# A hybrid block: spare banks for the last scores, one visit for the output projection, and block transposes moved from TensorE to VectorE and DRAM

## The chip, the cores and the metric

The kernel runs on one core of a Trainium2 chip. The metric is device microseconds of that core, from one launch; a time is the median of several runs. Five engines work beside each other, each with its own instruction queue: TensorE (PE in the profile; its weight loads are listed as PEld), VectorE (DVE), ScalarE (ACT), GpSimd (POOL) and SyncE (SP), which here only issues DMAs.

## The reference, cut to what matters

Input x has 2 sequences of 2048 tokens of 256 features, all float32. Four layers follow each other, each on the normalized x and added to it:

```python
x = x + attention_a(layernorm(x))   # 16 heads of 16 features, 4 for keys and values, softmax
x = x + ffn(layernorm(x))           # "rotations"
x = x + attention_b(layernorm(x))   # linear and causal, 16 heads, rotary, gate, norm, projection
x = x + ffn(layernorm(x))           # "rotations", the second time, the same weights
```

The core of attention_a is `softmax(q k / 4) v` and a projection `out @ Wo + bo`. The core of ffn is

```python
gf = global_net(x.mean(over tokens))          # one number a sequence
out = x
for _ in range(3):
    tf = coupling_net(out)                     # one number a token
    coupling = 0.1 + range * (0.7 * gf + 0.3 * tf - 0.5) * 2
    out = out + coupling * twist(out)
return out
```

So ffn needs its input feature by feature for the matmuls, and, before anything else can be scaled, the sum of its input over a sequence.

## The kernel before, in words

The tokens stay in SBUF as `xs`: 32 tiles of 128 tokens by 256 features. A second buffer, `zq` (128 partitions, 2 halves of the features, 4096 tokens), holds the transposed input of whatever layer needs it by features. The tokens are cut into 8 blocks of 512 (`NB`, `BLK`), four to a sequence.

**Attention a** (`attention_a`, from line 153) works in 32 units: block j and one of four groups of heads g. For a unit, `largest` (line 361) first computes all scores with queries on the partitions, 64 banks of 128x512 (`s`, line 376), and VectorE takes the maximum of each bank (line 380). Later the unit's scores are computed again with keys on the partitions (`p`, `score`, line 643), a second matmul subtracts the maxima (`shift`, line 649), ScalarE takes the exponential (line 655), and `weigh` (line 630) multiplies by the values. The generator `largest` runs 80 banks (`LEAD`) ahead of this second pass. The main loop (line 637) goes over 32 units x 16 steps kb; each step draws four banks of maxima from `largest` and handles four scores r = 0 to 3. PSUM has 8 banks: 3 for the maxima's `s` (pool `pss`), 4 for `p` (`psp`), 1 for the weighted sum (`pav`). As the maxima run ahead, they end before the second pass does, in unit 30 at kb = 12.

`finish(u, av)` (line 459) is a generator too: the loop calls it once a step (lines 667 and 684), and it handles the unit just ended, in small portions. For the last group of a block (g = 3) it ends with the output projection: two banks `po` of eight matmul records each (line 499), and VectorE's add to `xs` (line 504), with a `yield` after each bank, so that the two lie in two neighbouring steps.

**Behind it** (`behind`, line 721): first rotations, attention b, second rotations. All instructions of PE, VectorE, ScalarE and GpSimd keep the order of the program here (`in_order(begin)`, line 1419); the DMAs on SP are not bound by that. All PSUM tiles but one come from one pool of 7 banks (`bank`, line 740).

Attention b goes block by block (the loop from line 1329), software-pipelined by hand: x is the current block, y the next, `before` the previous. Each block has four quarters of 128 tokens: `energies(t)` multiplies keys and queries into four banks `pe` (line 1114) and VectorE masks them into `en` (line 1120); `output(t)` multiplies the state (line 1131) and then `en` by the values (line 1140). `project_out(h)` projects half a block, transposes it for statistics (`pog`, line 993) and lets VectorE compute them (lines 106 to 110); `add_out(h)` adds the result to `xs` (line 1180).

The inputs of the second rotations are made here too, one block late: `next_look` computes the normalization's statistics, `next_norm` (line 1188) writes the normalized tokens into `fzt`, and `next_turn` (line 1192) transposes them. `turn` (line 126) does this with eight PE transposes of 128x128 into two banks (line 131), and ScalarE copies each bank into `zq` while it adds the sum over the tokens into `sums1` (`accum_out`, line 1196; an activation and a read of the accumulator). `next_turn` of the previous block is the last thing in an iteration; the next thing on all engines is `x.energies(0)` of the next block. The last block's own `next_turn` comes after the loop.

`context(b)` (line 774), drawn by `next(front)` in iteration NB - 2 for the first sequence and by `next(front1)` behind the loop for the second, adds up `sums1` and computes the global network. The second rotations then read `zq`.

Of the kernel before, what the change touches and what calls it, by code (L numbers as in the profile page):

```python
# [9 lines left out]
F32 = mybir.dt.float32  # L10
F32R = mybir.dt.float32r
AF = mybir.ActivationFunctionType
# [4 lines left out]
P = 128  # L17
B, N, D = 2, 2048, 256
T = B * N
BLK = 512  # L20
NB = T // BLK
BPB = N // BLK
KB = N // P
# [44 lines left out]
def tile_hybrid(ctx: ExitStack, tc: tile.TileContext, x: bass.AP, consts: bass.AP, wa_d: bass.AP, wf_d: bass.AP, wb_d: bass.AP, out: bass.AP):  # L68
    nc = tc.nc
# [8 lines left out]
    zq = keep.tile([P, 2, T], F32, name="zq")  # L78

    own = ctx.enter_context(tc.tile_pool(name="own", bufs=1))  # L80
    dram = ctx.enter_context(tc.tile_pool(name="a_dram", bufs=2, space=bass.MemoryType.DRAM))
# [15 lines left out]
    def tokens(j):  # L97
        return xs[:, 4 * j : 4 * j + 4, :]
# [54 lines left out]
    def attention_a():  # L153
        with ExitStack() as st:
# [20 lines left out]
            pss = st.enter_context(tc.tile_pool(name="a_s", bufs=3, space=PSUM))  # L175
            psp = st.enter_context(tc.tile_pool(name="a_p", bufs=4, space=PSUM))
# [168 lines left out]
            units = [(j, g) for j in range(NB) for g in range(G)]  # L345
# [113 lines left out]
            def finish(u, av):  # L459

                j, g = units[u]
                m, e = g // 2, 64 * (g % 2)
                avs = own.tile([P, BLK], F32, tag="swap", name=f"avs{u}", bufs=2)
                nc.scalar.copy(avs, av)
                if g == 0:
                    tc.keep_in_program_order(
                        nc.gpsimd.tensor_tensor(
                            tokens(j), tokens(j), bo_row.unsqueeze(1).to_broadcast([P, 4, D]), ALU.add
                        )
                    )  # L470
                    outs[j] = [own.tile([P, 2, BLK], F32, tag=t, name=f"{n}{j}") for t, n in (("og", "oc"), ("kt", "sums"))]
                oc, sums = outs[j]

                ds, dr = (dram.tile([KV, BLK], F32, tag=t, name=f"{t}{u}") for t in ("ds", "dr"))
                nc.sync.dma_start(ds, avs[16:P:32, :])
                rs = own.tile([P, 16], F32, tag="rs", name=f"rs{u}", bufs=2)
                nc.sync.dma_start(rs, ds.rearrange("r (p x) -> (r p) x", x=16))
                for r in range(KV):
                    nc.sync.dma_start(oc[e + 16 * r : e + 16 * r + 16, m, :], avs[32 * r : 32 * r + 16, :])
                for _ in range(5):  # L480
                    yield
                tc.keep_in_program_order(nc.vector.reciprocal(rs, rs))
                nc.sync.dma_start(dr.rearrange("r (p x) -> (r p) x", x=16), rs)
                for r in range(KV):
                    nc.sync.dma_start(
                        sums[e + 16 * r : e + 16 * r + 16, m, :], dr[r : r + 1, :].to_broadcast([16, BLK])
                    )
                for _ in range(3):
                    yield
                if g % 2 == 1:  # L490
                    nc.gpsimd.tensor_tensor(oc[:, m, :], oc[:, m, :], sums[:, m, :], ALU.mult)  # L491
                yield
                if g == G - 1:
                    for i in range(2):
                        po = bank(f"po{j}_{i}")
                        for t in range(2):
                            tok = slice((2 * i + t) * P, (2 * i + t + 1) * P)
                            for h in range(2):
                                mm(  # L499
                                    po[:, t * D : (t + 1) * D], oc[:, h, tok], wo[:, h, :],  # L500
                                    start=(h == 0), stop=(h == 1),
                                )
                        pair = tokens(j)[:, 2 * i : 2 * i + 2, :]
                        nc.vector.tensor_tensor(pair, pair, po.rearrange("p (t d) -> p t d", t=2), ALU.add)
                        yield

            LEAD, WARM = 64 + 16, 6
            ahead = largest()
# [3 lines left out]
            at = {n: tuple(a - _WA["wk"][0] for a in _WA[n]) for n in ("wk", "bk", "wv", "bv")}  # L512
# [124 lines left out]
            for u, kb in ((u, kb) for u in range(len(units)) for kb in range(KB)):  # L637
                if (u, kb) == (0, 4):
                    in_order(begin, (engines.PE,))
                qP, mrow = queries[u], mrows[u % 2]  # L640
                k0 = units[u][0] // BPB * N + kb * P
                t, es = [], []

                def score(r):
                    row = slice(64 * (r % 2), 64 * (r % 2) + 64)
                    t.append(psp.tile([P, BLK], F32, tag="p", name=f"p{u}_{kb}_{r}"))
                    mm(t[r], kP[r // 2][row, k0 : k0 + P], qP[r // 2][row, :], start=True, stop=False)  # L647

                def shift(r):
                    row = slice(64 * (r % 2), 64 * (r % 2) + 64)  # L650
                    mm(t[r], pick[row, :], mrow[r // 2][row, :], start=False, stop=True)  # L651

                def exp(r):
                    es.append(sb.tile([P, BLK], F32, tag="e", name=f"e{u}_{kb}_{r}", bufs=8))
                    nc.scalar.activation(es[r], t[r], AF.Exp, scale=1.0 / HD**0.5)  # L655


                next(ahead, None)
                next(ahead, None)
                score(0)  # L660
                score(1)
                shift(0)
                shift(1)
                exp(0)
                exp(1)
                if kb == 1:
                    next(done, None)
                score(2)
                next(ahead, None)
                score(3)  # L670
                shift(2)
                next(ahead, None)
                shift(3)
                exp(2)
                exp(3)
                if last is not None:
                    if last[1] == 0:
                        av = pav.tile([P, BLK], F32, tag="av", name=f"av{last[0]}")
                    weigh(*last)
                    if last[1] == KB - 1:  # L680
                        done = finish(last[0], av)
                last = u, kb, es
                if kb > 1:
                    next(done, None)
                    next(norms, None)
                if u % G == 1 and kb == 1 and G < u < 4 * G:
                    norms = norm(u // G - 1)
                if kb == 4 and u + 2 < len(units):
                    project(u + 2)()
                if rest is not None and next(rest, "end") == "end":  # L690
                    rest = None
                    loads.close()
                    late = later_pools["late"] = ctx.enter_context(tc.tile_pool(name="late", bufs=1, side="right"))
                    for n, (name, of) in enumerate((("wf", wf_d), ("wb", wb_d))):
                        weights[name] = late.tile([P, of.shape[1]], F32, name=name)
                        nc.sync.dma_start(weights[name], of)
                    for name in ("w4", "b3"):
                        at = slice(*_WF[name])
                        nc.sync.dma_start(weights["wf"][64:P, at], wf_d[0:64, at])
# [21 lines left out]
    def behind(tail):  # L721
        wf, wb = weights["wf"], weights["wb"]
        late = later_pools["late"]
# [199 lines left out]
        sums1 = hold.tile([P, 2, NB], F32, name="sums1")  # L923
# [72 lines left out]
        class Block:  # L996
# [19 lines left out]
            def turn(self):  # L1016
                j = self.j
                self.z = take("z", [P, 2, BLK], f"bz{j}")
                turn(self.zt, lambda c: bank(f"bztr{j}_{c}"), lambda c, tr: nc.scalar.copy(self.z[:, c, :], tr))
# [170 lines left out]
                scale(self.fzt, self.tile_of, *self.scales)  # L1190

            def next_turn(self):
                j = self.j
                turn(
                    self.fzt, lambda c: bank(f"ztr1_{j}_{c}"),
                    lambda c, tr: nc.scalar.activation(
                        zq[:, c, j * BLK : (j + 1) * BLK], tr, AF.Copy, accum_out=sums1[:, c, j : j + 1]
                    ),
                )


        blocks = [Block(j) for j in range(NB)]
# [21 lines left out]
        f = rotations(0, sums0, False)  # L1224
        context, first, second, third, fourth, _ = f
# [100 lines left out]
        f = rotations(1, sums1, True)  # L1326
        context, first, second, third, fourth, turn_ahead = f
        front, front1 = context(0), context(1)
        for j, x in enumerate(blocks):
# [28 lines left out]
            x.energies(2)  # L1358
            if before:
                before.next_norm()  # L1360
            if j == NB - 2:
                next(front)
            if y:
# [35 lines left out]
        fourth(0)  # L1399
        first(2, 1)  # L1400
        third(1)
        x.next_turn()
        next(front1)
        second(2)
# [134 lines left out]
```

## Time and profile before

| what | us |
|---|---|
| median of 3 runs (2105.64 to 2108.85) | 2107.24 |
| the profiled execution | 2107.98 |
| its span, first to last instruction | 2106.2 |
| PE busy | 2085.9 |
| DVE busy | 1697.6 |
| ACT busy | 1427.5 |
| POOL busy | 355.2 |

The profile comes from one execution. Its busy times overlap, as the engines work beside each other; matmuls are pipelined, so that PE counts as busy in small waits too. The granted TensorE clock was 0.997 over the span. In time, attention a takes the span up to about 1510 us, the first rotations up to about 1695 (the first projection for attention b is at 1682), attention b from there to about 1955, and the second rotations the rest. Lines of a timeline give start, duration, engine, line, operation, tiles (out<-in), shapes and how many were merged; in brackets, how long the engine had been idle and who ended that. A group's duration in such a line is from its first start to its last end.

### The profile page before, as it was taken

Reading aid. Unit: us, or ns where it says so; the run is one execution under the profiler, and the core shown is the slowest. Engines: PE = TensorE matmul, PEld = TensorE weight load, DVE = VectorE, ACT = ScalarE, POOL = GpSimd, SP = SyncE. Lnnn points to the kernel's source line nnn. Section 1 sums busy time; section 2 is a strip of 40 time slices with the busy share of each in tenths; the row PEclk is TensorE's granted clock in tenths of the full one; section 3 lists DMA queues with packets and bytes.
Section 4 is the critical chain, followed back from the end, with each engine's and each line's share of the span. In section 5 each row is a group of like instructions: output and inputs, shape, how many; then the busy total and the mean of one; then the engine's idle time right before and its main releaser. Section 6 shows DMA issues by size and latency. Waiting matters only on the chain.

```text
span 2106.2 us, 38754 instructions
## 1 busy us (share of the span) xinstructions
PE 2085.9 (99%) x14158; PEld 1011.4 (48%) x14158; DVE 1697.6 (81%) x3241; ACT 1427.5 (68%) x2787; POOL 355.2 (17%) x352
## 2 busy tenths in 40 slices
PE   9999999999999999999999999999999999999998
PEld 4444444444444444444444444444444567776434
DVE  7999988998998998999899899987134678886336
ACT  4477777777777777787777777778864445554443
POOL 3100010000001000000000000000135355542451
PEclk9999999999999999999999999999999999999999
DMA  6511010110101011010110101100100000000002
GB/s 199 149 44 40 18 37 19 48 38 19 38 18 48 10 50 37 18 48 10 47 40 18 43 15 47 40 17 8 53 1 1 0 2 1 1 1 2 1 0 80
DMA packets 59696, 68.72 MB, mean 33 GB/s; under 512 B 24944, under 2 KB 34032, under 8 KB 59248
## 3 DMA queue, kind: packets, MB, share of 16 engines
q1 hardware_dynamic: 58592, 64.79, 11.2%
q8 instruction: 111, 1.82, 0.4%
q10 hardware_dynamic: 720, 0.92, 0.1%
q14 instruction: 81, 0.66, 0.1%
q0 software_dynamic: 192, 0.52, 0.1%
HBM read 35.78 MB, written 26.21 MB: 29 GB/s over the span
## 4 chain that ended last, share of the span: by engine, by line
PE 95%; DVE 2%; DMA 1%; ACT 1%; issue 0%; POOL 0%; SPq 0%; DVEq 0%; ACTq 0%; POOLq 0%
PE av L632 24%; PE s L376 23%; PE p L647 12%; PE q1f L814 8%; PE p L651 7%; PE q2f L824 4%; PE pe L1114 2%; PE bpo L1140 2%; PE po L499 1%; PE pq L972 1%; PE pw L981 1%; PE pv L981 1%; PE pk L972 1%; PE q3f L836 1%; PE pq L336 1%; DVE mx L380 1%
## 5 line engine op out<-in xcount | busy, mean ns | idle before, releaser
L380 DVE TENSOR_REDUCE mx<-s 128x1 f32<-128x512 f32 x2048 | 1273.7, 682 | 104.5 <-PE s L376 97.7
L655 ACT ACTIVATE e<-p 128x512 f32<-128x512 f32 x2048 | 1057.5, 603 | 314.1 <-PE p L651 307.4
L376 PE MATMUL s<-a_kP,qP 64*128 64x512 f32 x2048 | 706.5, 470 | 3.9 <-DVE mx L380 2.0
L651 PE MATMUL p<-a_m,a_pick 64*128 64x512 f32 x2048 | 585.3, 415 | 0.0
L376 PEld LDWEIGHTS s<-a_kP,qP 64*128 64x128 f32 x2048 | 283.6, 184 | 566.1 <-DVE mx L380 528.2
L632 PE MATMUL av<-e,a_v 128*32 128x512 f32 x4096 | 545.9, 605 | 0.0
L647 PE MATMUL p<-qP,a_kP 64*128 64x512 f32 x2048 | 525.7, 394 | 2.5 <-ACT e L655 2.5
L647 PEld LDWEIGHTS p<-qP,a_kP 64*128 64x128 f32 x2048 | 286.7, 185 | 65.2 <-ACT e L655 25.4
L651 PEld LDWEIGHTS p<-a_m,a_pick 64*128 64x128 f32 x2048 | 283.7, 184 | 25.8
L814 PE MATMUL q1f<-zq,wf 128*128 128x512 f32 x384 | 176.1, 601 | 0.0
L632 PEld LDWEIGHTS av<-e,a_v 128*32 128x32 f32 x4096 | 81.0, 108 | 128.6 <-issue 120.5
L398 POOL TENSOR_TENSOR mt<-nm,mt 128x16 f32<-128x16 f32 x31 | 6.9, 221 | 733.7 <-ACT mt L397 733.7
L815 ACT ACTIVATE a1f<-q1f,wf 128x512 f32<-128x512 f32 x96 | 65.8, 686 | 94.6 <-PE q1f L814 91.4
L814 PEld LDWEIGHTS q1f<-zq,wf 128*128 128x128 f32 x384 | 70.2, 190 | 96.9 <-issue 85.3
L1120 DVE TENSOR_TENSOR en<-pe,small 128x512 f32<-128x512 f32 x128 | 79.4, 681 | 15.0 <-PE pe L1114 15.0
L855 DVE TENSOR_SCALAR cf<-cf,f_beta,alphaf 128x512 f32<-128x512 f32 x32 | 32.7, 1023 | 67.6 <-ACT cf L854 67.6
L824 PE MATMUL q2f<-a1f,wf 128*128 128x512 f32 x192 | 87.0, 595 | 0.0
L237 POOL TENSOR_TENSOR ql<-zq,qh 128x512 f32<-128x512 f32 x15 | 19.3, 1284 | 364.6 <-ACT qh L234 364.6
L859 POOL TENSOR_TENSOR tf<-cf,zq 128x512 f32<-128x512 f32 x32 | 56.6, 1768 | 102.4 <-DVE cf L855 101.9
L826 ACT ACTIVATE a2f<-q2f,wf 128x512 f32<-128x512 f32 x48 | 32.6, 685 | 56.2 <-PE q2f L824 56.2
L861 POOL TENSOR_TENSOR zq<-zq,tf 128x512 f32<-128x512 f32 x32 | 56.8, 1776 | 2.5
L491 POOL TENSOR_TENSOR oc<-oc,sums 128x512 f32<-128x512 f32 x16 | 20.6, 1288 | 209.6 <-DMA sums<-dr 138.2
(209 smaller groups left out, 1634.3 us busy)
## 6 DMA issues: line engine op xcount, KB each, us to landing
qP<-dq SPq DMA_DIRECT2D x64, 256.0 KB
dq<-qh SPq DMA_DIRECT2D x62, 128.0 KB
dq<-ql SPq DMA_DIRECT2D x62, 128.0 KB
a_kP<-dk SPq DMA_DIRECT2D x16, 256.0 KB
oc<-avs SPq DMA_DIRECT2D x128, 32.0 KB
sums<-dr SPq DMA_DIRECT2D x128, 32.0 KB
out<-xs SPq DMA_DIRECT2D x16, 256.0 KB
xs<-in_x SPq DMA_DIRECT2D x7, 512.0 KB
```

What stands on the lines that cost most here:

```text
L376: mm(s, qP[r // 2][row, qi * P : (qi + 1) * P], kP[r // 2][row, k0 + kb * BLK : k0 + (kb + 1) * BLK], start=True, stop=True,)
L380: nc.vector.tensor_reduce(mx[:, r, qi : qi + 1, kb], s, AX.X, ALU.max)
L632: mm(av[32 * r : 32 * r + 32, :], vA[:, units[u][0] // BPB * KB + kb, 32 * r : 32 * r + 32], es[r], start=(kb == 0), stop=(kb == KB - 1),)
L647: mm(t[r], kP[r // 2][row, k0 : k0 + P], qP[r // 2][row, :], start=True, stop=False)
L651: mm(t[r], pick[row, :], mrow[r // 2][row, :], start=False, stop=True)
L655: nc.scalar.activation(es[r], t[r], AF.Exp, scale=1.0 / HD**0.5)
L814: mm(q1, w1[:, c, m * P : (m + 1) * P], z[:, c, :], start=(c == 0), stop=(c == 1))
L815: nc.scalar.activation(a1[:, m, :], q1, AF.Gelu, bias=b1[:, m : m + 1])
L824: mm(q2, w2[:, c, :], a1[:, c, :], start=(c == 0), stop=(c == 1))
L859: nc.gpsimd.tensor_tensor(t1, cs, z[:, 0, :], ALU.mult)
L861: nc.gpsimd.tensor_tensor(z[:, 1, :], z[:, 1, :], t1, ALU.subtract)
L1120: nc.vector.tensor_tensor(self.ens[t][w], pes[w].rearrange("p (h n) -> p h n", h=4), const("triu").unsqueeze(1).to_broadcast([P, 4, P]), A ...
```

## The change

Three edits. First, the `yield` after each bank `po` of the output projection moves out of the loop, so that both banks are done in one step. Second, once the maxima are done, the scores with odd r take their bank from the maxima's pool. Third, for the blocks 0 to 6, `next_turn` no longer uses PE: VectorE transposes 128 tokens by 256 features in squares of 32x32 within one instruction; 16 DMAs (one per 128 tokens and 32 partitions) write the squares to a DRAM tile in the right places, in runs of 32 elements; two DMAs bring it back into `zq`. The squares lie in a ring of three buffers. The sums over the tokens, which came with ScalarE's copy out of the banks, are now made by a ScalarE copy of `zq` onto itself, `next_sum`, one iteration later (for block 6 behind the loop). Block 7 is transposed as before.

```diff
@@ finish @@
                         nc.vector.tensor_tensor(pair, pair, po.rearrange("p (t d) -> p t d", t=2), ALU.add)
-                        yield
+                    yield
@@ score @@
-                    t.append(psp.tile([P, BLK], F32, tag="p", name=f"p{u}_{kb}_{r}"))
+                    spare = r % 2 == 1 and LEAD + 4 * (u * KB + kb) >= 64 * len(units)
+                    pool, tag = (pss, "s") if spare else (psp, "p")
+                    t.append(pool.tile([P, BLK], F32, tag=tag, name=f"p{u}_{kb}_{r}"))
@@ Block @@
             def next_turn(self):
                 j = self.j
+                if j + 1 < NB:
+                    to = dram.tile([D, BLK], F32, tag="dz", name=f"dz{j}")
+                    at = to.rearrange("(b f) (t a i) -> t a f b i", f=32, a=4, i=32)
+                    for t in range(4):
+                        square = late.tile([P, D], F32, tag="square", name=f"square{j}_{t}", bufs=3)
+                        nc.vector.transpose(square, self.fzt[:, t, :])
+                        for a in range(4):
+                            nc.sync.dma_start(
+                                at[t, a], square[32 * a : 32 * a + 32, :].rearrange("f (b i) -> f b i", i=32)
+                            )
+                    for c in range(2):
+                        nc.sync.dma_start(
+                            zq[:, c, j * BLK : (j + 1) * BLK], to[c * P : (c + 1) * P, :]
+                        )
+                    return
                 turn(
...
+            def next_sum(self):
+                for c in range(2):
+                    z = zq[:, c, self.j * BLK : (self.j + 1) * BLK]
+                    nc.scalar.activation(z, z, AF.Copy, accum_out=sums1[:, c, self.j : self.j + 1])
@@ the loop over the blocks of attention b @@
             if before:
                 before.next_norm()
+            if j > 1:
+                blocks[j - 2].next_sum()
@@ behind that loop @@
         third(1)
+        blocks[NB - 2].next_sum()
         x.next_turn()
```

## The prediction

> **What bounds the kernel now.** I read the page first: the busy rows, then the chain that ended last.
>
> ```profile
> PE   9999999999999999999999999999999999999998
> DVE  7999988998998998999899899987134678886336
> PE 95%; DVE 2%; DMA 1%; ACT 1%; issue 0%; POOL 0%; SPq 0%; DVEq 0%; ACTq 0%; POOLq 0%
> ```
>
> The chain is TensorE (PE) almost throughout, so work taken from PE pays, but a wait added to VectorE (DVE) costs only where PE then waits for it. A busy PE in these rows can hide waits, so I read the three stages in the timeline.
>
> Behind the last maxima (1464 to 1510 us), an inner step alternates:
>
> ```profile
> 1464.76 4.18 ACT L655 ACTIVATE e<-p 128x512 f32<-128x512 f32 x8
> 1466.06 0.50 PE L647 MATMUL p<-qP,a_kP 64*128 64x512 f32 x2
> 1466.87 0.18 PEld L647 LDWEIGHTS p<-qP,a_kP 64*128 64x128 f32 x1 [0.29 <-ACT e L655]
> 1468.52 0.50 PE L647 MATMUL p<-qP,a_kP 64*128 64x512 f32 x2
> 1469.35 4.18 ACT L655 ACTIVATE e<-p 128x512 f32<-128x512 f32 x8 [0.41 <-PE p L651]
> 1470.64 0.50 PE L647 MATMUL p<-qP,a_kP 64*128 64x512 f32 x2
> ```
>
> Steps start 2.46 and 2.12 us apart (the step before these starts at 1463.94, 2.12 earlier). In the long one the third score waits for a bank that the exponentials still hold; then ScalarE (ACT) idles 0.41.
>
> The output projection, here for one batch of tokens:
>
> ```profile
> 1370.43 2.00 PE L499 MATMUL po<-a_wo,oc 128*128 128x256 f32 x8
> 1372.36 0.51 PE L376 MATMUL s<-a_kP,qP 64*128 64x512 f32 x2
> 1372.47 0.69 DVE L504 TENSOR_TENSOR xs<-xs,po 128x512 f32<-128x512 f32 x1 [1.72 <-PE po L499]
> 1373.81 0.18 PEld L376 LDWEIGHTS s<-a_kP,qP 64*128 64x128 f32 x1 [0.42 <-DVE mx L380]
> ```
>
> PE works 1.93 us on a visit, and DVE, which had to wait for po, then makes the step lose more.
>
> The turn from one block of attention b to the next, on PE, and then on DVE:
>
> ```profile
> 1792.53 0.60 PE L993 MATMUL pog<-small,og 128*128 128x128 f32 x4
> 1792.96 1.04 PE L131 MATMUL ztr<-small,zt 128*128 128x128 f32 x8
> 1793.93 1.24 PE L1114 MATMUL pe<-qeo,rotk 32*128 32x256 f32 x16
> 1799.62 1.08 PE L1140 MATMUL bpo<-en,b_veo 128*32 128x128 f32 x32
> ```
>
> ```profile
> 1794.18 0.17 DVE L110 TENSOR_SCALAR rs_bo<-mv_bo 128x2 f32<-128x2 f32 x1
> 1795.09 2.48 DVE L1120 TENSOR_TENSOR en<-pe,small 128x512 f32<-128x512 f32 x4 [0.75 <-PE pe L1114]
> 1797.50 0.86 DVE L1180 SCALAR_TENSOR_TENSOR xs<-pw,rs_bo,xs 128x256 f32<-128x256 f32 x2
> ```
>
> The eight transposes hold PE for 0.97 us (1792.96 to 1793.93). DVE is free from about 1794.3, and its four en, done at 1797.57, are wanted by PE at 1799.62: 2 us of cover.
>
> How fast small transfers go, in SP's queue:
>
> ```profile
> 800.27 1.82 SPq L407 DMA_DIRECT2D dm<-mr  x4
> 803.23 1.16 SPq L412 DMA_DIRECT2D a_m<-dm  x4
> ```
>
> Four issues take 1.82 us (1.70 in another unit; median 0.42 each), and the fourth is landed 1.14 us after its issue.
>
> **The change, part by part.**
>
> *One visit.* From PE's av (L632) before the first po to that after the second, the trace goes 1369.44, 1374.24, 1379.04: 4.80 a step against 2.71 without po, so a visit costs 2.10, of which 1.93 is PE's work and 0.17 DVE's late start. Merged, the work stays (3.86) and the 0.17 is paid once. Seven batches lie in the loop; the eighth ran behind it in one go already. Gain 7 x 0.17 = 1.2 us. The second po takes one more of four banks; its add ends 0.11 + 0.69 = 0.80 after the step's start, while the fourth score comes 1.0 after, so no new wait. Bounds: 0 (the add is late after all) to 2.
>
> *Maxima's banks.* Half of the scores move to the three banks that the maxima leave, from unit 30, kb 12: 20 steps. Then no score waits for the four exponentials just before it. A step without that wait is 2.11 us (PE), and ACT needs 4.18/2 = 2.09, so PE sets 2.115. Now 19 intervals run from 1463.94 to 1507.68, 2.302 each. Gain 19 x 0.187 = 3.5. Bounds: 0 to 3.6 (2.302 - 2.11 over 19). What follows needs all exponentials anyway, so nothing new is late there.
>
> *Transposes.* Seven turns (blocks 0 to 6) lose their 0.97 on PE: 6.8 us. In their place each turn puts four DVE transposes, 16 writes and two loads on SP; later two in-place ACT copies, 0.59 each, with the sums' reads. These replace two like them (L1196: 592 and 202 ns) and stand before the gates; ACT idles 4.06 us before L1051 in each block, so I take 0. Without that cover the gates' banks come free late, 0.5 us a block at most by the distance from the gates' end (1812.22 + 1.6) to the next pe (1813.64). SP has nothing else queued in this stage but these, and its loads' result is wanted a block later. POOL's queue is not touched.
>
> The catch: there are three square buffers and four squares. The fourth transpose must wait until all four writes of the first have landed, and behind it on DVE stand the four en that PE wants. Count from T = 1794.27, when DVE ends its statistics:
> - A square: the trace has 128x32 at 0.20 (L403), and a 128x512 shuffle at 0.63 from one start to the next (1893.26, 1893.89). Between these by columns: 0.40.
> - Four issues: 1.75 by dm, which also moves 32 partitions in runs of 128 B.
> - Landing: 1.14 by dm, and 0.2 more because each write has 256 runs where dm has 32: 1.3. dm and its like take 10 to 15 ns a packet of one engine (4.2% of 16 engines in 3 us for 192 packets), 0.2 us for 256 over 16, below the issue time, so the engines do not become the limit.
> - The fourth square ends at T + 0.40 + 1.75 + 1.3 + 0.40 = T + 3.85. The last en is done 2.48 later, T + 6.33, and PE has 13/16 of L1140's 1.01 left: it ends at T + 7.15.
> - Unhindered, PE would start L1140 at 1799.62 - 0.97 = T + 4.38 and end at T + 5.39.
>
> So PE stalls 1.76 and has won 0.97: each turn loses 0.8. DVE then lags by about 1.4 us, and has it back by the block's end, where it idles 0.91 + 1.31 before L106 and L1180. Six turns have such a successor (the seventh is followed by the rotations): 6 x 0.8 - 0.97 = +3.8.
>
> Bounds, per turn. Low: squares 0.20, issues 0.35 (dr, L483), landing 1.07 (dr): fourth ends T + 2.87, stall 0.78, net -0.2; the part gives -2. High: squares 0.63, issues 0.59 (dq, L246), landing 2.8 (longest wait for dm): T + 6.4, net +3.4; the part gives +19. I stay with dm, the nearest row.
>
> The last square set: 16 issues x 0.44 from 1955.8, landing, two loads and their landing, end near 1966.5; its sums are taken at about 1968. That is covered, by little.
>
> *Weighed against the trace.* dr writes 64 B runs and lands 1.07 us after its issue, dm 1.14. [...] The eight transposes cost PE 0.97 here. [...]
>
> **Sum.** Own time of the profiled execution 2107.98 (span 2106.2, 1.8 around it): -1.2 - 3.5 + 3.8 = -0.9, so 2107.1. The median of the runs shown is 0.74 below that execution, so I predict 2106.4 on it: no change. About 0.2% (4.2 us) is what can be told from no change.
>
> **Rivals.**
> - *The wait is not felt* (faster): PE keeps its 6.8, and the sum is -11.5, or about -8.5 if ACT's copies hold the gates' banks 0.5 us in six blocks: 2096 to 2099. It needs the fourth square to end before T + 2.1. For it: DVE has 2 us of cover. Against: four issues alone take 1.4 to 1.8.
> - *SP and landing are slower than dm* (slower): the writes have 256 runs of which I have no row. With 0.59 an issue, as dq, and 1.94 to land (the most that ds takes, 1477.05 to 1478.99), the fourth ends at T + 5.1, a turn loses 2.0, the part costs 11: 2114. It decides the other way from T + 4.7 on (net 1.65 a turn takes up the 4.7 of the other parts and 4.2 more).
> - *The first two parts bring nothing*, since a bank is chosen that comes no sooner: 2111.
>
> **Chances.** Forecast 0.44, its own range 2100 to 2111; not felt 0.22; slower DMA 0.28; the third 0.06. Of the forecast's, 0.12 lie over 4.2 below, 0.29 within, 0.03 above; the third gives 0.04 within and 0.02 above. So faster 0.34, same 0.33, slower 0.33. Range 2097 to 2117: it takes in most of the first rival and of the second, and leaves out the ends of both.
>
> **What would show it.** The fourth square waits on DVE for the writes of the first, 1 to 3 us, in every turn; L1140 of a block's first quarter starts late and names en; blocks in this stage get longer by 0.5 to 1 us instead of shorter by 1. Exponentials between 1464 and 1507 run without the 0.41 gaps. L499 shows seven groups of 16 in the loop. If DVE's transposes are followed at once by en, the first rival holds; if SP's issues are 0.6 or more, the second.

## The result, and the profile after

The changed kernel takes 2117.27 us (median of 4 runs, 2114.33 to 2120.02) beside 2106.97 for the kernel before: ratio 1.0048, interval 1.0036 to 1.0060. It is slower by some 10 us. The forecast was 2106.4, no change, with 2117 as the range's upper end. The profiled execution took 2116.64, its span is 2114.9. One execution of e6_two_buffers below, the profiled one, took 5652.77 us and is left out of every number here. In the changed kernel the lines behind the first two edits are numbered three higher (L1140 becomes L1143).

The busy row of PE, in 40 slices, is digit for digit that of before. The chain that ended last and DVE's busy row do show something (lines of the page):

```profile
PE 91%; DVE 5%; DMA 1%; ACT 1%; issue 1%; POOL 1%; SPq 0%; DVEq 0%; ACTq 0%; POOLq 0%
DVE  7999989998998998999899899896143877886336
```

PE had 95% of the chain and DVE 2%; now 4% of the chain, some 85 us, has passed from PE to others, mostly to DVE. A chain share isn't a loss, but it says which engine to look at.

**Lengths of the stages.** Up to the last maximum (DVE's last L380) the start times of the executions differ by up to 5 us, whatever the kernel: 1463.6 us in one of before, 1458.9 to 1463.8 in the others. So all comparisons below are made inside stages, from start times in the traces. "Visits" is the sum of seven stretches of four inner steps of attention a, one around each batch's projection (from PE's av one step ahead of it). "Last scores" runs from the last L380 to the first q1f (a rotation's network runs through q1f, a1f, q2f, a2f and so on in turn, q on PE and a on ACT; p1f is the first matmul of the global network), "blocks" from the first pe to the end of the last L1143 (L1140 in before), "tail" from there to the end.

| profiled execution | visits | last scores | blocks | tail |
|---|---|---|---|---|
| before | 106.38 | 48.02 | 248.08 | 157.83 |
| after | 104.50 | 44.72 | 257.51 | 162.71 |
| difference | -1.88 | -3.30 | +9.43 | +4.88 |

The differences add up to +9.1 of the measured 10.3. The stage between "last scores" and "blocks" is 188.7 in both. The stretches of "visits" leave out one thing: behind the second visit, at 493.06 us, the granted clock is one half for 3.4 us, and the ten steps from the one ahead of that visit take 34.77 us, 1.44 more than around the first and third. Seven of the ten traces with the merged visit have one such dip behind one of the first three visits; the two traces with separate visits (before, e4_squares) have none there. With it the sum is +10.6.

*Last scores.* ACT, in the timeline behind the last maximum, and PE's av beside it:

```profile
1462.43 10.54 ACT L658 ACTIVATE e<-p 128x512 f32<-128x512 f32 x20
```

```profile
1462.73 1.06 PE L632 MATMUL av<-e,a_v 128*32 128x512 f32 x8
...
1464.85 1.06 PE L632 MATMUL av<-e,a_v 128*32 128x512 f32 x8
```

Twenty exponentials follow each other without the 0.41 gaps, and steps come every 2.12 us instead of 2.46 and 2.12 in turn.

*One visit.* `po` is now one group of 16 on PE, 3.72 us at 1368.54, with no wait between its banks; so it is in all seven batches.

```profile
1368.54 3.72 PE L499 MATMUL po<-a_wo,oc 128*128 128x256 f32 x16
```

*A turn*, the first one, on DVE, PE and SP. T, the end of DVE's statistics, is 1756.89:

```profile
1756.89 1.09 DVE L1204 STREAM_TRANSPOSE square<-zt 128x256 f32<-128x256 f32 x3
1760.59 0.45 DVE L1204 STREAM_TRANSPOSE square<-zt 128x256 f32<-128x256 f32 x1 [2.60 <-DMA dz<-square]
1760.96 2.45 DVE L1123 TENSOR_TENSOR en<-pe,small 128x512 f32<-128x512 f32 x4
```

```profile
1760.76 0.61 PE L1134 MATMUL bpo<-rotq,state 128*128 128x128 f32 x4
1761.66 0.41 PE L1143 MATMUL bpo<-en,b_veo 128*32 128x128 f32 x2 [0.30 <-DVE en L1123]
...
1763.46 1.06 PE L1143 MATMUL bpo<-en,b_veo 128*32 128x128 f32 x26 [0.19 <-DVE en L1123]
1764.45 1.15 PE L1117 MATMUL pe<-qeo,rotk 32*128 32x256 f32 x16
```

```profile
1757.36 7.71 SPq L1206 DMA_DIRECT2D dz<-square  x16
```

Three squares run at once; the fourth waits 2.60 us, and en behind it. PE's stall hardly shows as idle time (four gaps of 0.2 to 0.3): L1143 is drawn out from 1.08 to 2.86 us, because it starts with the first en and then goes at DVE's pace. It shows in the distance from a block's first pe to its second: 6.70 before (6.25 in one block), and 8.75, 8.79, 8.79, 8.86, 8.89, 8.77 after. All seven waits together (us in all, times, the longest):

```profile
DVE square L1204 <- DMA dz<-square: 18.1, 7, 2.8
```

*The tail.* DVE, ACT and PE behind the last block, with the seventh turn:

```profile
1963.07 0.45 DVE L1204 STREAM_TRANSPOSE square<-zt 128x256 f32<-128x256 f32 x1 [2.76 <-DMA dz<-square]
1963.44 0.83 DVE L1183 SCALAR_TENSOR_TENSOR xs<-pw,rs_bo,xs 128x256 f32<-128x256 f32 x2
```

```profile
1967.47 2.07 ACT L124 ACTIVATE zt<-xs,nb_f,rs_f 128x256 f32<-128x256 f32 x4 [7.74 <-POOL nb_f L119]
1969.45 1.24 ACT L818 ACTIVATE a1f<-q1f,wf 128x512 f32<-128x512 f32 x2
```

```profile
1970.17 1.98 PE L817 MATMUL q1f<-zq,wf 128*128 128x512 f32 x4 [1.16 <-ACT a1f L818]
...
1980.86 0.61 PE L786 MATMUL p1f<-gmf,wf 128*128 128x1 f32 x4 [2.18 <-DVE gmf L782]
```

Read across: the fourth square's wait holds back add_out, this the statistics of next_look (from 1964.19), these the norm on ACT, and behind the norm stands a1f, on which PE's q1f waits. ACT sat idle 7.74 us ahead of that norm, 3.46 in before, where PE stood still neither ahead of q1f nor ahead of p1f (before, ACT and then PE):

```profile
1960.27 2.07 ACT L124 ACTIVATE zt<-xs,nb_f,rs_f 128x256 f32<-128x256 f32 x4 [3.46 <-POOL nb_f L119]
```

```profile
1964.10 3.70 PE L814 MATMUL q1f<-zq,wf 128*128 128x512 f32 x8
...
1974.26 0.61 PE L783 MATMUL p1f<-gmf,wf 128*128 128x1 f32 x4
```

### The profile page after: what moved, and what is told of

The parts are those of the page before. It is cut to its first block, busy times and chain, and to the rows that moved or that the text cites. A ratio compares the mean times of both kernels' runs of the same rounds, so it can differ in the third digit from the quotient of the medians.

```text
span 2114.9 us, 38893 instructions
## 1 busy us (share of the span) xinstructions
PE 2084.5 (99%) x14102; PEld 1006.7 (48%) x14102; DVE 1704.5 (81%) x3269; ACT 1426.6 (67%) x2787; POOL 355.1 (17%) x352
## 4 chain that ended last, share of the span: by engine, by line
PE 91%; DVE 5%; DMA 1%; ACT 1%; issue 1%; POOL 1%; SPq 0%; DVEq 0%; ACTq 0%; POOLq 0%
PE av L632 24%; PE s L376 22%; PE p L650 11%; PE q1f L817 8%; PE p L654 7%; PE q2f L827 4%; PE bpo L1143 1%; PE po L499 1%; PE pw L984 1%; PE pv L984 1%; PE pe L1117 1%; PE pq L336 1%; PE q3f L839 1%; PE pk L975 1%; DVE mx L380 1%; DVE en L1123 1%
## 5 line engine op out<-in xcount | busy, mean ns | idle before, releaser
L380 DVE TENSOR_REDUCE mx<-s 128x1 f32<-128x512 f32 x2048 | 1272.6, 682 | 106.1 <-PE s L376 100.4
```

The source lines that it names most:

```text
L380: nc.vector.tensor_reduce(mx[:, r, qi : qi + 1, kb], s, AX.X, ALU.max)
```

## The experiments

**Theory:** the loss is the fourth square's wait for a buffer, in six turns by en, in the seventh by next_look and ACT's queue. **Rivals:** the transfers, ACT's extra copies or DVE's own 1.7 us of transposes make it; or part comes from the first two edits, or from the granted clock.

All kernels in one table; "blocks" and "tail" as above, from the profiled execution. The ratio isn't taken from the two medians and can lie 0.0004 beside theirs; e6_two_buffers counts three executions.

| kernel | median us | of before beside it | ratio (interval) | blocks | tail |
|---|---|---|---|---|---|
| e1_visit_banks | 2101.54 | 2106.10 | 0.9976 (0.9967 to 0.9986) | 248.07 | 157.82 |
| e4_squares | 2121.30 | 2106.10 | 1.0070 (1.0057 to 1.0083) | 257.50 | 162.94 |
| e5_slots | 2105.46 | 2106.10 | 0.9993 (0.9985 to 1.0002) | 245.26 | 164.38 |
| e7_last_on_pe | 2111.30 | 2106.10 | 1.0026 (1.0017 to 1.0035) | 258.88 | 158.07 |
| e6_two_buffers | 2136.23 | 2107.80 | 1.0138 (1.0122 to 1.0153) | | |
| e11_two_again | 2135.54 | 2105.73 | 1.0140 (1.0110 to 1.0169) | 276.33 | 163.00 |
| e8_slots_six | 2100.28 | 2107.80 | 0.9965 (0.9953 to 0.9978) | 245.29 | 158.07 |
| e9_late_fourth | 2099.16 | 2107.80 | 0.9960 (0.9944 to 0.9975) | 243.62 | 157.55 |
| e10_late_six | 2099.42 | 2107.80 | 0.9961 (0.9949 to 0.9974) | 243.65 | 158.08 |
| e12_visit_banks_again | 2105.26 | 2109.17 | 0.9983 (0.9974 to 0.9992) | 248.07 | 157.83 |
| e13_late_fourth_again | 2100.70 | 2109.17 | 0.9959 (0.9947 to 0.9972) | 243.63 | 157.55 |

### The parts alone

e1_visit_banks is the kernel before with the first two hunks of the diff, e4_squares with the others.

> The kernel before with the merged visit and the spare banks alone. Theory (these two parts work as they were meant to, and the turns alone lost the time): first q1f starts 5.6 us earlier than in the kernel before, as in the changed kernel, and nothing behind it differs, so -5.6 us, about 2101.4 and a ratio of 0.9973. Rival (part of the loss behind the first rotations comes from these two parts, by the place where the later stages start or by a lower granted clock): the 5.6 us are partly gone by the end, -3 us or less.

Measured -4.6 us, and in the trace "visits" 104.48 and "last scores" 44.73, as in the changed kernel; blocks and tail are those of before to 0.01. By this trace the two parts cost nothing behind the first rotations: the rival falls. The whole run once more, beside the late fourth square of below:

> The merged visit and the spare banks alone, once more, now beside the version with the late fourth square. By the lengths of the stages in the traces the two parts bring 1.9 and 3.3 us: -5.2 us, ratio 0.9975.

-3.9 us, and its stages are the same again. The stages give -5.2; both intervals hold it. This trace has the dip behind a visit (at 673.53), e1_visit_banks' has none (the mean granted clock is 0.996 here and 0.997 there); that its 1.4 us are what the medians lack is not shown.

> The kernel before with the transposes by VectorE and DRAM alone. Theory (the wait of the fourth square for the first square's writes): every block behind a turn 1.57 us longer, six times 9.4, and 4.9 in the tail as in the changed kernel: +14.3 us, 2121.3, ratio 1.0068. Rival (the tail's 4.9 is a chance of the granted clock in the one execution that was profiled): +9.4 to +11, 2117 to 2118.

Measured +15.2; blocks 9.42 longer, tail 5.11 longer. So the transposes by squares make all of the loss, and the tail's part of it is no chance of one execution.

### The wait taken away

e5_slots keeps the number of transposes, writes, loads and copies, and gives the squares other room:

```diff
-                        square = late.tile([P, D], F32, tag="square", name=f"square{j}_{t}", bufs=3)
+                        square = self.fzt[:, t - 1, :] if t else late.tile([P, D], F32, tag="square", name=f"square{j}")
```

> The changed kernel, but only the first square has a buffer of its own: squares 2, 3 and 4 are written into the quarter of zt that the square before them has just read, so that no square waits for a transfer; the same number of transposes, writes, loads and copies. Theory (the loss is the wait for a buffer): no wait of a DMA ahead of a square, L1143 of the first quarter unhindered; four squares take DVE 1.7 us, inside the 2 us of cover. A turn then wins 0.88 on PE and loses at most 0.23 by DVE's lag: six times 0.65 to 0.88 gained instead of 1.57 lost, -13.3 to -14.7 us against the changed kernel, and in the tail next_look comes 2.8 us earlier, so that most of the 4.9 goes as well: 2098 to 2101. Rival (transfers, ACT's extra copies or VectorE's own work of 1.7 us make the loss): 2112 or more.

Measured 2105.5, between the two. The trace says why. In the blocks the theory holds: the squares follow each other at once, and en follows them (DVE, first turn).

```profile
1756.98 0.44 DVE L1204 STREAM_TRANSPOSE square<-zt 128x256 f32<-128x256 f32 x1
1757.52 1.54 DVE L1204 STREAM_TRANSPOSE zt<-zt 128x256 f32<-128x256 f32 x3
1758.99 2.45 DVE L1123 TENSOR_TENSOR en<-pe,small 128x512 f32<-128x512 f32 x4
```

The first pe to the second takes 6.61 to 6.83 us behind a turn, and the blocks are 12.25 us shorter than in the changed kernel, with all its transfers and copies still there. But the tail is 6.55 longer than before's. My edit had brought a new wait: zt has one buffer, and block 7's norm, which follows the seventh turn closely, must now wait until the 12 writes out of zt have landed; the other four leave the first square's own buffer (ACT):

```profile
1956.96 2.07 ACT L124 ACTIVATE zt<-xs,nb_f,rs_f 128x256 f32<-128x256 f32 x4 [9.41 <-DMA dz<-zt]
```

In the blocks the same wait isn't felt, since the next norm comes some 14 us after the turn begins. The prediction for this run failed by that; the theory of the six turns did not.

### The seventh turn

e7_last_on_pe turns block 6 by TensorE; the copies of its sums go.

```diff
-                if j + 1 < NB:
+                if j + 1 < NB - 1:
...
-        blocks[NB - 2].next_sum()
```

> The changed kernel, but block 6 is turned by TensorE as block 7 is, with its sums from the evacuation: six turns by squares, none behind the last block. Theory (the seventh turn's wait holds back add_out, next_look and, over ACT's queue, a1f): the tail is as in the kernel before, so the 4.9 us that were lost behind block 7's outputs are gone and the six turns' loss stays: 2112.4 on the median of the changed kernel, ratio to the kernel before 1.0025. Rival (the tail's loss is the granted clock, whatever the seventh turn does): 2115 to 2117.

Measured 2111.3. The tail is 158.07, 4.64 shorter than in the changed kernel and 0.24 longer than before's, with the blocks' loss still there (258.88; 1.37 more than in the changed kernel, as a dip of the clock, a mean of 0.79 over 1825 to 1833, fell into one block). So what was lost behind the last block came by the seventh turn.

e8_slots_six has this edit and that of e5_slots.

> Squares 2 to 4 in the quarters of zt as in e5_slots, and block 6 turned by TensorE as in e7_last_on_pe. In e5_slots the outputs of block 7 were done 8.39 us earlier than in the kernel before, and 6.6 were lost behind them, where ScalarE's next norm waited 9.4 us for the writes out of zt. Theory: with no seventh turn by squares nothing is lost there: 2106.1 - 8.4 = 2097.7, ratio 0.996. Rival (the loss behind the last block has to do with less work for TensorE in the blocks or with the clock): 2101 or more.

Measured -7.5 us (2100.28), with the tail at 158.07 instead of 164.38: the 6.3 us that e5_slots had lost there are back.

### Only the order changed

e9_late_fourth keeps three buffers, all transfers and all copies. The fourth square, its writes and the loads come behind the next block's first energies, so that en isn't queued behind the wait; in the tail they come behind next_look.

```diff
-                    for t in range(4):
+                    self.squares(range(3))
...
             x.energies(0)
+            if j > 1:
+                blocks[j - 2].squares([3])
             if before:
                 before.add_out(1)
...
         x.next_look()
+        blocks[NB - 2].squares([3])
```

> The changed kernel with its three buffers, but the fourth square, its writes and the two loads are issued behind the next block's first energies (in the tail: behind next_look). Nothing is left out and no buffer is added. Theory (the wait counts only because en stands behind it): the writes have landed when the fourth square comes, so no wait; en is 1.3 us later than without squares, inside the cover of 2: each of six turns wins 0.88 less at most 0.23; in the tail next_look is not held back, what stays there is about 1.2 us of the extra copies on ScalarE ahead of a2f: 2106.1 - 5.65 - 4 to -5 + 0 to 1.2 = 2095.5 to 2098. Rival (DVE's own four transposes, 1.7 us, make the stall): 2106 or more.

Measured -8.6 us. A wait of 0.24 is left, in nobody's way: en, four of them from 1759.27, is done ahead of it (DVE, then PE, in the first turn). In the tail ACT sat idle 4.54 ahead of its norm, not 7.74.

```profile
1761.95 0.45 DVE L1216 STREAM_TRANSPOSE square<-zt 128x256 f32<-128x256 f32 x1 [0.24 <-DMA dz<-square]
```

```profile
1762.65 1.08 PE L1143 MATMUL bpo<-en,b_veo 128*32 128x128 f32 x32
1763.66 1.15 PE L1117 MATMUL pe<-qeo,rotk 32*128 32x256 f32 x16
```

L1143 runs in one piece of 1.08 again. The blocks take 243.62, 4.46 less than before's and 13.89 less than the changed kernel's. This is the strongest run for the theory: all the work is there and only its order differs. It also settles ACT's copies: with all of them in place the tail is 0.28 shorter than before's, and what they cost there is at most the one gap left, 0.43 us of PE ahead of p1f.

e10_late_six is the same with block 6 on TensorE.

> As e9_late_fourth, and block 6 is turned by TensorE. Theory: six turns win as in e9_late_fourth, the tail is that of the kernel before: 2106.1 - 5.65 - 4 to -5 = 2095.5 to 2096.5, ratio 0.995 to 0.9955. If e9_late_fourth has lost nothing behind the last block, this one is 0.9 slower than it.

Measured -8.4 us; no difference from e9_late_fourth that the medians could tell, 0.53 in the tail by the traces.

> The version with the late fourth square, once more. By the lengths of the stages six turns bring 4.5 us more than the first two parts alone and the tail 0.3: -9.9 us against the kernel before, ratio 0.9953, and 4.7 us below the visit and the banks alone. Rival (the stages hide a loss elsewhere): the two are alike within 2 us.

Measured -8.5 us, and 4.6 below the visit and the banks alone, run beside it. So the turns by squares do bring a gain once nothing waits behind them, and this version beats both kernels.

### The wait made longer

e6_two_buffers has `bufs=2` instead of 3.

> The changed kernel with two square buffers instead of three: the same transposes, writes, loads and copies. Theory (the wait for a buffer is the loss): the third square waits for the first's four writes and the fourth for the second's, four issues of 0.45 later than now, 1.8 us more in each of the six turns and about as much behind the seventh: 6 x 1.8 + 1.8 = 12.6 us more than the changed kernel, about 2129, ratio 1.011. Rival (the transfers or the extra work of VectorE and ScalarE as such): no difference from the changed kernel, 2116 to 2118.

Measured +28.4 against before (29.5 with the long execution in the median), 18 to 19 more than the changed kernel instead of 12.6. The kernel ran again, for a profile of an ordinary execution.

> The same kernel as e6_two_buffers, for a profile at an ordinary clock. It took 29.5 us more than the kernel before, 19 more than the changed kernel, where 12.6 were expected. Theory: the waits ahead of squares 3 and 4 add up to more than one run of four issues a turn, because the third square's writes are issued only after the wait, and the fourth square's wait for the second's writes is then followed by en: stalls of PE of 4 to 5 us in each of the six turns, 2 to 3 more than now, and 3 to 5 more behind the last block. Rival: the stalls grow by 1.8 as expected, and the rest comes from somewhere else, such as a lower granted clock behind the longer pauses.

Measured +29.8. Two waits a turn now, 2.92 and 1.43 in the first turn (DVE):

```profile
1759.80 0.45 DVE L1204 STREAM_TRANSPOSE square<-zt 128x256 f32<-128x256 f32 x1 [2.92 <-DMA dz<-square]
1761.68 0.45 DVE L1204 STREAM_TRANSPOSE square<-zt 128x256 f32<-128x256 f32 x1 [1.43 <-DMA dz<-square]
```

In this turn the first pe to the second takes 10.62 us, 1.87 more than in the changed kernel: the four further issues, as expected. In the other five it takes 11.23 to 11.71. There the granted clock falls (behind each of these turns its mean over 8 us is 0.59 to 0.79, behind the first 1.00); in the second turn it stretches L1143's last 26 matmuls on PE from 1.06 to 1.91 us:

```profile
1799.74 1.91 PE L1143 MATMUL bpo<-en,b_veo 128*32 128x128 f32 x26 [0.19 <-DVE en L1123]
```

So the rival named for this run holds: of the blocks' 18.8 us over the changed kernel, 6 x 1.8 = 10.8 are the wait, and the other 8 come in the blocks in which the clock falls. The block without a dip is 1.87 longer, the five with one 2.53 to 4.05. The tail is only 0.3 longer (163.00), where 1.8 and then 3 to 5 were expected: ahead of q1f PE now waits 3.13 instead of 1.16, but ahead of p1f only 0.55 instead of 2.18.

## Why the prediction was wrong, point by point

- **One visit:** right within the stretches. -1.88, predicted -1.2 within 0 to 2. But the gain isn't the even 0.17 a batch of the sum: the first three batches gain 0.12 each, the last four 0.38, which was not followed up. The dip of the clock behind a visit, 1.4 to 1.5 us in seven of ten traces, was in no term; why it comes is open.
- **Maxima's banks:** right. -3.30, predicted -3.5.
- **The wait of the fourth square:** right in mechanism, in every turn, and named in advance; its size was short. PE's stall has a mean of 2.18, predicted 1.76. In the first turn, term by term: the first write is issued 0.47 after T, not 0.40; four issues take 1.80 (median 0.449), not 1.75; the landing 1.43, not 1.3; the square 0.45, not 0.40. That is 0.30. L1143 ends 1.1 after the last en, where I had 0.82 left of it. PE wins 0.88 by the transposes, not 0.97, and four of the blocks lose another 0.23 at their projection, where I had DVE recovered (block 6 loses 0.69). Net 1.57 a turn, predicted 0.8; six turns +9.43 instead of +4.8. The bounds, -0.2 to +3.4, held it.
- **The seventh turn:** this is the step that failed. I wrote that it is "followed by the rotations", took it as a pure gain of 0.97 and asked only when its data would be wanted ("covered, by little"). It cost 4.88, an error of 5.85 us, the larger part of the miss. The chain was in the listed order of the tail: behind the fourth square on DVE stand add_out and next_look, behind that on ACT the norm, behind the norm a1f. I had named what is queued behind the wait for the six turns (en) and not for the seventh. The pieces seen there: PE idle 1.16 and 2.18, and q1f at half clock 1.64 longer, against 0.97 won; that is 4.0 of the 4.9. The rest I have not followed to its end.
- **ACT's copies at no cost:** right in the six turns by e9_late_fourth, at most 0.43 in the tail.
- **The rival of slower DMA**, at 2114, is near in time and wrong in its reason: the median issue is 0.449 and the wait ends 1.43 after the fourth, not 0.59 and 1.94.

Summed by these steps: -1.9 - 3.3 + 9.4 + 4.9 = +9.1 instead of -0.9.

## What to carry to other kernels

In these runs a wait cost what stood behind the waiting instruction on its engine (en, with the blocks 9.43 us longer; next_look, with the tail 4.88 longer): list that queue for each place where the instruction occurs, above all for the last one, whose successors differ. The ring, with one buffer fewer than the burst of four squares, made the last square wait for the first one's writes, 2.60 us in the first turn; if no buffer fits, put the last piece behind the work that others wait for, which here was worth 18 us without any change of work. After taking a wait away, look for where the memory that it guarded is used next: e5_slots moved the wait from a square to a norm (9.41 us).

## What the runs showed of the hardware

**PE's granted clock was halved behind some pauses of 2.18 to 3.13 us.** In the tail of the changed kernel, PE resumes at 1980.86 after the pause of 2.18. The granted clock (third number from the end) in windows of 1 us:

```profile
1981.00:1982.00 1.00, 1.00 (x5) 0.81 (x6) 0.85 (x2) 0.26 (x1) 0.76 (x1) 0.64 0.00 0
1982.00:1983.00 1.00, 1.00 (x2) 0.34 (x1) 0.00 (x0) 0.00 (x0) 1.00 (x1) 0.50 0.00 0
1983.00:1984.00 1.00, 1.00 (x2) 0.34 (x1) 0.96 (x2) 0.00 (x0) 0.92 (x2) 0.50 0.00 0
```

In the next two windows it is 0.66 and 1.00: it is one half from 1981.27 to 1984.69, 3.41 us, and eight q1f take 5.34 instead of 3.70. Such a dip (a mean of 0.79 over 8 us) also follows pauses of 2.20 in e5_slots and of 2.37 and 3.13 in e11_two_again, and one lies in the tail of e4_squares (1984 to 1992). None (a mean of 1.00 over 8 us) follows the pause of 1.16 in the tail of the changed kernel, one of 2.17 in e11_two_again and one of 2.83 in e5_slots. In e7_last_on_pe a dip comes after a stall in pieces, the longest 0.88. Before, between 1701 and 2090 us, has neither such a pause nor a dip (a mean of 1.00). So pauses of 2.2 were enough here, but not every time, and what decides it was not shown. Nor was it for the dips in attention a: ahead of the one from 493.06 to 496.47 PE idles only 0.40 and 0.25.

**Costs that the trace of before did not hold.** In the changed kernel DVE transposes a 128x256 tile in squares in 0.42 us (median of 28), and a write of 32 KB in runs of 128 B takes 0.45 to issue (median of 112) and, in the first turn, lands 1.43 later.
